# A DiT block in fp32: the projection's seven sums in a ring of two-bank tiles, its rows stored by GpSimd, weight operations spread over groups, three casts on ScalarE

## The chip, the cores and the metric

The program runs on one core of a Trainium2 chip. The metric is device time in microseconds, the median of the runs. Before the change it is 3237.1 us (three runs, 3235.74 to 3239.63). Lower is better.

## The reference

A transformer block with adaptive layer norm. `x` is (2, 2048, 576) in fp32, the conditioning is (2, 576); there are 16 heads of 36 dimensions and an MLP of width 2304.

```python
mod = jax.nn.silu(c) @ w_ada + b_ada
sh_msa, sc_msa, g_msa, sh_mlp, sc_mlp, g_mlp = jnp.split(mod, 6, axis=1)
xn = _ln(x, 1e-06) * (1 + sc_msa[:, None, :]) + sh_msa[:, None, :]
qkv = (xn @ w_qkv + b_qkv).reshape(B, N, 3, H, hd)
q, k, v = _ln(qkv[:, :, 0], ...), _ln(qkv[:, :, 1], ...), qkv[:, :, 2]
attn = softmax(einsum('bqhd,bkhd->bhqk', q, k) * hd ** -0.5)
o = einsum('bhqk,bkhd->bqhd', attn, v).reshape(B, N, C)
x = x + g_msa[:, None, :] * (o @ w_proj + b_proj)
xn2 = _ln(x, 1e-06) * (1 + sc_mlp[:, None, :]) + sh_mlp[:, None, :]
m = gelu(xn2 @ w1 + b1) @ w2 + b2
x = x + g_mlp[:, None, :] * m
```

## The kernel before

For each of the two batches the kernel runs three stages in turn: the QKV product (`inputs`, sixteen tiles of 128 tokens), attention (`attend`) and the output projection (`outputs`). Then one MLP runs over both batches. In the trace batch 0 has its attention until 1034 us and its projection from there to 1139; batch 1 has its projection from 2140 to 2229, and the MLP follows.

**Attention** walks over 8 pairs of heads (p), 4 blocks of 512 queries (qb) and 4 groups of keys (g). Each step of about 6 us makes scores (L1225), their exponentials on ScalarE (L1229) and the product with the values (L1238). VectorE takes that product out of PSUM (L1286 for the first group, L1288 for the others), which frees the bank for the next scores, and at the end of a query block divides by the sums: L1257 is the reciprocal, L1258 the product with it. Work for other stages hangs on this loop as *hooks*, functions called at a given (p, qb, g). `residual_begun` is one: at g = 3 of each query block from p = 3 on, GpSimd adds the gated bias to one tile of `x` and stores it to `x1_dram` (L1409, L1412, L1413). `output_weights` is another: it loads `w_proj`, and three hooks at p = 5 let GpSimd multiply the weights by the gate (`gated`, L1320 and L1323), make three sums (`summed`, L1326 to L1328) and two differences (`differed`, L1331, L1332). A hook only decides the place of its instructions in GpSimd's order.

**Projection.** Eight pairs of token tiles are worked one after the other with Strassen's scheme: a pair's 256 tokens by 512 features against the 512 by 576 weights, in seven products (`product`, L1435) in place of eight, and the last 64 features apart (`last_product`, L1441). GpSimd makes the sums of token blocks that the products need (`pair_summed`, L1371 and L1373), two pairs ahead, in two sets of memory. The products land in three PSUM tiles: `four` of four banks, `two` of two banks and `one` of one bank (two buffers). VectorE adds them into the pair's rows in SBUF, which hold the residual from `residual` (L1427, a load by GpSimd from `x1_dram`): L1458, L1465, L1466, L1467, L1470 and L1479. `inner` are the two middle quarters of the rows and `outer` the first and last. Then SP stores the rows to `x1_dram` (L1480). In batch 0 the rows have five scratch tiles, in batch 1 three, because there the place holds the last 64 rows of `w1`.

In batch 0 five tiles of the finished rows are also normalised and transposed for the MLP: `rows_measured` (L272 to L278) in one pair, L1460 in the next, in place, and the transpose L998 after it. SP loads the weights of batch 1's QKV in this stage (`kept_weights`, L970 to L974). In batch 1 the MLP's work comes in between (`placed`): four sums of weights on VectorE (`weight_sums`, L1663 to L1666), the splitting of the last weight rows into a rounded part and its rest (`last_parts`; `weight_parts`, L400 and L401), and the modulation of tiles (L1020, L388, L389 on ScalarE and L390 on GpSimd).

**Order.** A planner orders the instructions of each engine by its own costs, except inside `manual_schedule`, where program order holds for the engines named: TensorE everywhere in this path, VectorE and GpSimd in attention and in the projection. Semaphores guard what is shared, by tile.

Of the kernel before, what the change touches and what calls it, by code (L numbers as in the profile page):

```python
# [31 lines left out]
def dit_block(  # L32
# [364 lines left out]

    def weight_parts(dst, src):

        nc.vector.tensor_copy(dst[0:64], src)  # L400
        nc.vector.tensor_tensor(dst[64:128], src, dst[0:64].bitcast(F32), ALU.subtract)  # L401
# [350 lines left out]
    def block_of_small():  # L752
# [547 lines left out]
        def output_weights(b):  # L1300
# [16 lines left out]

            def gated():
                for k in range(FULL):
                    nc.gpsimd.tensor_tensor(wp[:, k, :], wp[:, k, :], g1, ALU.mult)  # L1320
                for a in range(2):
                    r = slice(64 * a, 64 * a + 64)
                    nc.gpsimd.tensor_tensor(wp4[r, 0, :], wp4[r, 0, :], g1[r, a * HALF : (a + 1) * HALF], ALU.mult)  # L1323

            def summed():
                nc.gpsimd.tensor_tensor(sums[1], sums[2], sums[5], ALU.add)  # L1326
                nc.gpsimd.tensor_tensor(sums[6], sums[2], sums[3], ALU.add)
                nc.gpsimd.tensor_tensor(sums[7], sums[4], sums[5], ALU.add)  # L1328

            def differed():  # L1330
                nc.gpsimd.tensor_tensor(sums[3], sums[3], sums[5], ALU.subtract)  # L1331
                nc.gpsimd.tensor_tensor(sums[4], sums[4], sums[2], ALU.subtract)  # L1332

            return (sums, wp4[:, 0, :]), (gated, summed, differed), close

# [79 lines left out]
        def outputs(b, weights, memory, between, scratch, turned_of=lambda t: None):  # L1415
# [17 lines left out]
            def product(out, tokens, i, start=True):  # L1433
                for k in range(2):
                    nc.tensor.matmul(  # L1435
                        out[:, :HALF], tokens[:, k, :], sums[i][:, k, :], start=start and k == 0, stop=k == 1
                    )

            def last_product(out, tokens, a):
                r = slice(64 * a, 64 * a + 64)  # L1440
                nc.tensor.matmul(out[:, :HALF], tokens[r], last[r], start=True, stop=False)  # L1441
# [3 lines left out]
            for p in range(pairs):  # L1445
                q00, q01, q10, q11, a, c = pair_blocks(p)
                s = memory[p % 2]
                four = psum["q"].tile([P, 4, 512], F32, tag="q", name="four")
                two = psum["m"].tile([P, 2, 512], F32, tag="m", name="two")
                one = psum["r"].tile([P, 512], F32, tag="r", name="one")  # L1450
                y = rows[p].rearrange("p t (a f) -> p (t a) f", a=2)
                inner, outer = y[:, 1:3, :], y[:, 0::3, :]
                placed(2 * p)
                last_product(four[:, 2, :], a, 1)
                last_product(four[:, 1, :], c, 0)
                product(four[:, 2, :], q00, 3, False)
                product(four[:, 3, :], s[2], 2)
                nc.vector.tensor_tensor(inner, four[:, 2:4, :HALF], inner, ALU.add)  # L1458
                for turn, x1, scales in to_turn:
                    nc.vector.tensor_scalar(x1, x1, *scales, ALU.subtract, ALU.mult)  # L1460
# [9 lines left out]
                nc.vector.tensor_tensor(outer, one[:, :HALF].unsqueeze(1).to_broadcast([P, 2, HALF]), outer, ALU.add)  # L1470
                last_product(two[:, 0, :], s["last"], 0)
                last_product(two[:, 1, :], s["last"], 1)
                product(two[:, 0, :], s[7], 7, False)
                product(two[:, 1, :], s[6], 6, False)
# [5 lines left out]
                nc.sync.dma_start(out=rows_of(x1_dram, p), in_=rows[p])  # L1480
                for i in range(2):
# [15 lines left out]
        for b in range(B):  # L1497
# [77 lines left out]
            close_psum()  # L1575
            close_psum = opened_psum(q=1, m=1, r=2)
            wp, _, close_wp = opening["wp"]
            if b + 1 < B:
# [8 lines left out]
                with tc.manual_schedule(engines={mybir.EngineType.DVE, mybir.EngineType.Pool}):  # L1587
# [64 lines left out]
        for j in range(TPB + 1):  # L1652
# [335 lines left out]
```

## Time and profile before

| What | us |
|---|---|
| Median of three runs | 3237.1 |
| The profiled execution | 3235.03 |
| Its span | 3233.1 |
| TensorE busy | 3145.1 |
| VectorE busy | 1564.9 |
| ScalarE busy | 1471.5 |
| GpSimd busy | 739.2 |

In the lines of the profile PE is TensorE's matmul, PEld its weight load, DVE VectorE, ACT ScalarE, POOL GpSimd and SP the engine that only issues DMAs; a "q" behind a name is the engine's sequencer. L1435 is line 1435 of the kernel. A line of waits reads "who, line, for whom: us in total, times, longest". A line of a timeline reads "start, duration, engine, line, operation, destination<-sources, count", and in brackets how long the engine had been idle before it and what ended that. The windows give each engine's busy time in a stretch, the granted TensorE clock (PEclk, 1.00 is full) and the share of DMA time used.

### The profile page before, as it was taken

Reading aid. Unit: us, or ns where it says so; the run is one execution under the profiler, and the core shown is the slowest. Engines: PE = TensorE matmul, PEld = TensorE weight load, DVE = VectorE, ACT = ScalarE, POOL = GpSimd, SP = SyncE. Lnnn points to the kernel's source line nnn. Section 1 sums busy time; section 2 is a strip of 40 time slices with the busy share of each in tenths; the row PEclk is TensorE's granted clock in tenths of the full one; section 3 lists DMA queues with packets and bytes.
Section 4 is the critical chain, followed back from the end, with each engine's and each line's share of the span. In section 5 each row is a group of like instructions: output and inputs, shape, how many; then the busy total and the mean of one; then the engine's idle time right before and its main releaser. Section 6 shows DMA issues by size and latency. Waiting matters only on the chain.

```text
span 3233.1 us, 46806 instructions
## 1 busy us (share of the span) xinstructions
PE 3145.1 (97%) x17489; PEld 1852.9 (57%) x17489; DVE 1564.9 (48%) x2205; ACT 1471.5 (46%) x2843; POOL 739.2 (23%) x998
## 2 busy tenths in 40 slices
PE   7999999999999699999999999998999999999999
PEld 5873333333333478633333333346888888777777
DVE  6653434444445446434344454346566544454454
ACT  2326666666665023366666656641555652000000
POOL 4640000102212345300001121124333420111121
PEclk9999999999999899999999999999999999999999
DMA  5753222222222556511122212245544533433331
GB/s 151 167 97 83 79 61 51 65 58 63 69 75 59 176 119 124 94 40 39 42 58 70 66 50 72 74 135 169 165 135 136 141 113 114 148 129 113 117 103 38
DMA packets 312598, 311.96 MB, mean 96 GB/s; under 512 B 189865, under 2 KB 243305, under 8 KB 310249
## 3 DMA queue, kind: packets, MB, share of 16 engines
q1 hardware_dynamic: 256320, 201.62, 21.6%
q0 software_dynamic: 40656, 100.16, 12.0%
q10 hardware_dynamic: 15384, 7.08, 0.8%
q8 instruction: 141, 2.31, 0.3%
q14 instruction: 97, 0.79, 0.1%
HBM read 191.80 MB, written 106.45 MB: 92 GB/s over the span
## 4 chain that ended last, share of the span: by engine, by line
PE 92%; DVE 3%; DMA 2%; issue 2%; SPq 0%; ACT 0%; POOL 0%; DVEq 0%; POOLq 0%; ACTq 0%
PE b L1238 28%; PE b L1225 18%; PE s L1900 15%; PE m L1740 11%; PE s L1100 11%; PE m L1754 2%; PE one L1740 2%; PE four L1435 2%; PE s L1102 1%; PE two L1435 1%; DMA qk<-turned_qk 1%; DVE den L1257 1%; DMA xt<-in_x_dram 0%; PE one L1435 0%; DVE ot L1258 0%
## 5 line engine op out<-in xcount | busy, mean ns | idle before, releaser
L1229 ACT ACTIVATE pt<-b 128x512 f32<-128x512 f32 x2048 | 1058.2, 608 | 514.2 <-PE b L1238 299.9
L1238 PE MATMUL b<-pt,vt 128*64 128x512 f32 x4096 | 943.9, 603 | 0.0
L1238 PEld LDWEIGHTS b<-pt,vt 128*64 128x64 f32 x4096 | 273.9, 138 | 591.2 <-issue 452.5
L1225 PE MATMUL b<-qm,km 32*128 32x512 f32 x4096 | 578.9, 616 | 12.0 <-DVE ot L1288 8.9
L1288 DVE TENSOR_TENSOR ot<-b,ot 128x512 f32<-128x512 f32 x192 | 132.7, 691 | 620.3 <-PE b L1238 620.3
L1225 PE MATMUL b<-qe,ke 16*128 16x512 f32 x2048 | 428.2, 791 | 2.6 <-DVE ke L857 2.6
L1100 PE MATMUL s<-wq,xnt 128*128 128x288 f32 x1536 | 403.5, 406 | 2.7 <-ACT xnt L395 2.1
L1225 PEld LDWEIGHTS b<-qm,km 32*128 32x128 f32 x4096 | 193.7, 185 | 291.2 <-ACT pt L1229 211.6
L1900 PE MATMUL s<-ws,as 128*128 128x288 f32 x1440 | 351.8, 406 | 0.0
L1100 PEld LDWEIGHTS s<-wq,xnt 128*128 128x128 f32 x1536 | 280.4, 190 | 65.0 <-ACT xnt L395 1.6
L1900 PEld LDWEIGHTS s<-ws,as 128*128 128x128 f32 x1440 | 273.6, 190 | 75.6
L1257 DVE RECIPROCAL den<-den 128x512 f32<-128x512 f32 x64 | 213.6, 3337 | 2.2 <-DMA den<-den_dram 2.1
L1740 PE MATMUL m<-xnt,wb 128*128 128x256 f32 x864 | 210.9, 380 | 2.8 <-DVE cs L1774 2.8
L1740 PE MATMUL m<-s,wb 128*128 128x256 f32 x864 | 211.0, 380 | 0.0
L1003 POOL DMA_DIRECT2D turned<-squares x212 | 142.6, 679 | 287.7 <-DVE squares L998 281.1
L1286 DVE COPY ot<-b 128x512 f32<-128x512 f32 x64 | 44.3, 692 | 278.8 <-PE b L1238 278.8
L1740 PEld LDWEIGHTS m<-s,wb 128*128 128x128 f32 x864 | 165.0, 191 | 22.8
L1225 PEld LDWEIGHTS b<-qe,ke 16*128 16x128 f32 x2048 | 109.3, 185 | 118.6 <-issue 113.5
L1740 PEld LDWEIGHTS m<-xnt,wb 128*128 128x128 f32 x864 | 159.2, 190 | 22.2 <-DVE cs L1774 3.0
L812 POOL DMA_DIRECT2D km<-qk x56 | 28.1, 502 | 582.0 <-PE b L1225 576.9
L1409 POOL DMA_DIRECT2D spare<-in_x_dram x32 | 17.5, 548 | 609.6 <-DVE met L791 609.6
L1778 ACT ACTIVATE cs<-cs,b_sb 128x512 f32<-128x512 f32 x144 | 98.8, 719 | 114.3 <-DVE cs L1773 92.3
(242 smaller groups left out, 3153.4 us busy)
## 6 DMA issues: line engine op xcount, KB each, us to landing
gelu<-cs SPq DMA_DIRECT2D x144, 256.0 KB
hidden<-gelu SPq DMA_DIRECT2D x16, 2304.0 KB
qk<-turned_qk SPq DMA_DIRECT2D x120, 144.0 KB
qm<-qk SPq DMA_DIRECT2D x256, 64.0 KB
den<-den_dram SPq DMA_DIRECT2D x128, 128.0 KB
turned<-squares POOLq DMA_DIRECT2D x212, 72.0 KB, 2.6
xnt<-turned POOLq DMA_DIRECT2D x54, 256.0 KB, 4.0
spare<-in_x_dram POOLq DMA_DIRECT2D x35, 288.0 KB, 3.1
```

Of the source, the lines that this page charges most:

```text
L1003: queue.dma_start(out=by_square[g], in_=squares[g * SQ : (g + 1) * SQ, :].rearrange("p (k j) -> p k j", j=SQ))
L1100: nc.tensor.matmul(out_a, full[:, k, :], wq[:, k, f], start=k == 0, stop=False)
L1225: nc.tensor.matmul(ps, k[r, keys], q[r, :], start=first, stop=not first)
L1229: nc.scalar.activation(pt[:, h, :], banks[2 * c + h], AF.Exp, scale=SCALE)
L1238: nc.tensor.matmul(acc[64 * h : 64 * h + 64, :], vt[:, v0 : v0 + 64], pt[:, h, :], start=pt is pts[0][0], stop=pt is pts[-1][0],)
L1257: nc.vector.reciprocal(den, den)
L1288: nc.vector.tensor_tensor(ot, acc, ot, ALU.add)
L1435: nc.tensor.matmul(out[:, :HALF], tokens[:, k, :], sums[i][:, k, :], start=start and k == 0, stop=k == 1)
L1740: nc.tensor.matmul(out_m[m], wb[:, slot[m], k, f * P : (f + 1) * P], moving[m](k), start=k == 0 and m in (1, 2, 5, 6), stop=k == 1 and m == 1,
L1754: nc.tensor.matmul(out_m[m], wr[w][:, f * P : (f + 1) * P], a[:, i, t * PAIR : (t + 1) * PAIR], start=False, stop=i == 1 and m != 2,)
L1778: nc.scalar.activation(part, part, AF.Gelu, bias=b1_sb[:, g : g + 1])
L1900: nc.tensor.matmul(ms[m], stationary[m][:, f, :], ws[m][:, f, :], start=(f == 0), stop=(f == HF - 1))
```

## The change

It has four parts. The seven sums of a pair go into four PSUM tiles of two banks, `x`, `y`, `z`, `w`, from one pool of four that turns as a ring and stays open into the QKV product of the next batch; VectorE's six additions become eight, four of them half as wide. GpSimd stores the rows in place of SP. The eleven GpSimd operations on the projection's weights hang on eleven hooks at p = 5 and 6 in place of three. The first step of `weight_parts`, the cast, is done by ScalarE for the MLP's last weight rows.

```diff
-    def weight_parts(dst, src):
+    def weight_parts(dst, src, copy=nc.vector.tensor_copy):
-        nc.vector.tensor_copy(dst[0:64], src)
+        copy(dst[0:64], src)
         nc.vector.tensor_tensor(dst[64:128], src, dst[0:64].bitcast(F32), ALU.subtract)
...
+            making = [
+                *(lambda k=k: gated(k) for k in range(FULL)),
+                *(lambda a=a: last_gated(a) for a in range(2)),
+                lambda: combined(1, 2, ALU.add, 5),
+                lambda: combined(6, 2, ALU.add, 3),
+                lambda: combined(7, 4, ALU.add, 5),
+                lambda: combined(3, 3, ALU.subtract, 5),
+                lambda: combined(4, 4, ALU.subtract, 2),
+            ]
+            return (sums, wp4[:, 0, :]), making, close
...
-                four = psum["q"].tile([P, 4, 512], F32, tag="q", name="four")
-                two = psum["m"].tile([P, 2, 512], F32, tag="m", name="two")
-                one = psum["r"].tile([P, 512], F32, tag="r", name="one")
+                x, y, z, w = (s_tile() for _ in range(4))
...
+                def added(dst, part, op=ALU.add):
+                    nc.vector.tensor_tensor(dst, dst, part, op)
...
-                last_product(four[:, 2, :], a, 1)
-                last_product(four[:, 1, :], c, 0)
-                product(four[:, 2, :], q00, 3, False)
-                product(four[:, 3, :], s[2], 2)
-                nc.vector.tensor_tensor(inner, four[:, 2:4, :HALF], inner, ALU.add)
+                last_product(x[:, 0, :], a, 1)
+                last_product(y[:, 1, :], c, 0)
+                product(x[:, 0, :], q00, 3, False)
+                product(x[:, 1, :], s[2], 2)
+                added(inner, x[:, :, :HALF])
+                added(quarters[:, 3, :], x[:, 0, :HALF])
+                added(quarters[:, 3, :], x[:, 1, :HALF], ALU.subtract)
+                product(y[:, 0, :], s[5], 5)
+                product(y[:, 1, :], q11, 4, False)
                 for turn, x1, scales in to_turn:
                     nc.vector.tensor_scalar(x1, x1, *scales, ALU.subtract, ALU.mult)
                     turn(x1)
                 to_turn.clear()
-                product(four[:, 0, :], s[5], 5)
-                product(four[:, 1, :], q11, 4, False)
-                nc.vector.tensor_tensor(inner, four[:, 0:2, :HALF], inner, ALU.add)
-                nc.vector.tensor_tensor(outer, four[:, 1:3, :HALF], outer, ALU.add)
-                nc.vector.tensor_tensor(outer, outer, four[:, 0::3, :HALF], ALU.subtract)
-                product(one, s[1], 1)
+                added(inner, y[:, :, :HALF])
+                added(quarters[:, 0, :], y[:, 0, :HALF], ALU.subtract)
+                added(quarters[:, 0, :], y[:, 1, :HALF])
+                product(w[:, 0, :], s[1], 1)
                 placed(2 * p + 1)
...
+                added(outer, w[:, 0, :HALF].unsqueeze(1).to_broadcast([P, 2, HALF]))
+                last_product(z[:, 0, :], s["last"], 0)
+                last_product(z[:, 1, :], s["last"], 1)
+                product(z[:, 0, :], s[7], 7, False)
+                product(z[:, 1, :], s[6], 6, False)
...
-                nc.vector.tensor_tensor(outer, two[:, :, :HALF], outer, ALU.add)
-                nc.sync.dma_start(out=rows_of(x1_dram, p), in_=rows[p])
+                added(outer, z[:, :, :HALF])
+                nc.gpsimd.dma_start(out=rows_of(x1_dram, p), in_=rows[p])
...
-            hooks |= {(5, 1 + i, 1): lambda i=i: opening["wp"][1][i]() for i in range(3)}
+            hooks |= {
+                (5 + i // 6, 1 + i % 6 // 2, 1 + i % 2): lambda i=i: opening["wp"][1][i]() for i in range(11)
+            }
...
-            close_psum = opened_psum(q=1, m=1, r=2)
+            close_psum = opened_psum(s=4)
...
-                close_psum()
-                close_psum = opened_psum(s=4)
                 loaded[3] = tile_loaded(x[b + 1, 3 * P : 4 * P, :], nc.gpsimd)
...
-            lambda: weight_parts(wr[0], left),
-            lambda: weight_parts(wr[1], right),
+            lambda: weight_parts(wr[0], left, nc.scalar.copy),
+            lambda: weight_parts(wr[1], right, nc.scalar.copy),
             lambda: nc.vector.tensor_tensor(right, right, left, ALU.subtract),
-            lambda: weight_parts(wr[2], right),
+            lambda: weight_parts(wr[2], right, nc.scalar.copy),
```

More of the change, by code (lines that the diff above doesn't have):

```diff
@@ L1316, in output_weights, with gated, last_gated, combined @@
             }
[L1318 to L1334, printed above, removed]
+            def gated(k):
+                nc.gpsimd.tensor_tensor(wp[:, k, :], wp[:, k, :], g1, ALU.mult)
+            def last_gated(a):
+                r = slice(64 * a, 64 * a + 64)
+                nc.gpsimd.tensor_tensor(wp4[r, 0, :], wp4[r, 0, :], g1[r, a * HALF : (a + 1) * HALF], ALU.mult)
+            def combined(i, one, op, two):
+                nc.gpsimd.tensor_tensor(sums[i], sums[one], sums[two], op)
+            making = [
[8 more added lines that the diff above has]
+            return (sums, wp4[:, 0, :]), making, close
         def pair_memory():
@@ L1447, in outputs @@
                 s = memory[p % 2]
-                four = psum["q"].tile([P, 4, 512], F32, tag="q", name="four")
-                two = psum["m"].tile([P, 2, 512], F32, tag="m", name="two")
-                one = psum["r"].tile([P, 512], F32, tag="r", name="one")
-                y = rows[p].rearrange("p t (a f) -> p (t a) f", a=2)
-                inner, outer = y[:, 1:3, :], y[:, 0::3, :]
-                placed(2 * p)
-                last_product(four[:, 2, :], a, 1)
-                last_product(four[:, 1, :], c, 0)
-                product(four[:, 2, :], q00, 3, False)
-                product(four[:, 3, :], s[2], 2)
-                nc.vector.tensor_tensor(inner, four[:, 2:4, :HALF], inner, ALU.add)
+                x, y, z, w = (s_tile() for _ in range(4))
+                quarters = rows[p].rearrange("p t (a f) -> p (t a) f", a=2)
+                inner, outer = quarters[:, 1:3, :], quarters[:, 0::3, :]
+                def added(dst, part, op=ALU.add):
+                    nc.vector.tensor_tensor(dst, dst, part, op)
+                placed(2 * p)
+                last_product(x[:, 0, :], a, 1)
[7 more added lines that the diff above has]
+                product(y[:, 1, :], q11, 4, False)
                 for turn, x1, scales in to_turn:
@@ L1462, in outputs @@
                 to_turn.clear()
-                product(four[:, 0, :], s[5], 5)
-                product(four[:, 1, :], q11, 4, False)
-                nc.vector.tensor_tensor(inner, four[:, 0:2, :HALF], inner, ALU.add)
-                nc.vector.tensor_tensor(outer, four[:, 1:3, :HALF], outer, ALU.add)
-                nc.vector.tensor_tensor(outer, outer, four[:, 0::3, :HALF], ALU.subtract)
-                product(one, s[1], 1)
-                placed(2 * p + 1)
[L1470 to L1474, printed above, removed]
+                added(inner, y[:, :, :HALF])
+                added(quarters[:, 0, :], y[:, 0, :HALF], ALU.subtract)
+                added(quarters[:, 0, :], y[:, 1, :HALF])
+                product(w[:, 0, :], s[1], 1)
+                placed(2 * p + 1)
+                added(outer, w[:, 0, :HALF].unsqueeze(1).to_broadcast([P, 2, HALF]))
[3 more added lines that the diff above has]
+                product(z[:, 1, :], s[6], 6, False)
                 if p >= 1 and p + 2 < pairs:
```

## The prediction

> **What bounds the kernel now.** I read the page first (engines, then the chain that ended last), then TensorE's waits, then stage windows, then the timeline around each hole.
>
> ```profile
> PE 3145.1 (97%) x17489; PEld 1852.9 (57%) x17489; DVE 1564.9 (48%) x2205; ACT 1471.5 (46%) x2843; POOL 739.2 (23%) x998
> PE 92%; DVE 3%; DMA 2%; issue 2%; SPq 0%; ACT 0%; POOL 0%; DVEq 0%; POOLq 0%; ACTq 0%
> ```
>
> TensorE is the bound; no matmul is removed by the change, so it can win only what TensorE now stands idle (and the slow clock that follows idling). The stages in question are the two projections. The windows give duration and busy time by engine:
>
> ```profile
> core 0: us, PE busy (x) PEld busy (x) DVE busy (x) ACT busy (x) POOL busy (x), PEclk, DMA share, GB/s
> 1034.50:1139.20 104.70, 73.60 (x290) 47.50 (x289) 55.17 (x87) 8.72 (x23) 37.42 (x59) 0.89 0.59 174
> 2140.30:2228.50 88.20, 73.50 (x288) 47.52 (x289) 56.59 (x60) 12.19 (x30) 44.97 (x53) 0.96 0.47 162
> ```
>
> The waits inside the first, and then inside the second:
>
> ```profile
> DVE spare L1460 <- DMA x_dram<-spare: 23.9, 1, 23.9
> PE four L1441 <- issue: 19.7, 1, 19.7
> PE four L1435 <- DVE spare L1458: 9.5, 6, 3.4
> ...
> PE four L1435 <- DVE spare L1458: 11.5, 7, 3.6
> ```
>
> Two holes are seen. One: TensorE writes bank 0 of `four` only after VectorE has read banks 2 and 3 (L1458), in nearly every pair; the two are different banks, so it is the tile that is waited for. Two: one wait of 19.7 us, "issue" being no cause. The timeline names it:
>
> ```profile
> 1055.19 0.57 SPq L970 DMA_DIRECT2D wq<-wq_kept  x1
> 1059.26 22.09 SPq L1480 DMA_DIRECT2D x_dram<-spare  x2
> 1075.74 0.58 DVE L1460 TENSOR_SCALAR spare<-spare,mv,rstd 128x576 f32<-128x576 f32 x1 [23.91 <-DMA x_dram<-spare]
> 1079.33 1.42 PE L1441 MATMUL four<-wp,qo 64*128 64x288 f32 x4 [19.69 <-issue]
> ```
>
> Pair 0's rows (final at 1049.5, L1479) are stored from SP behind 5184 KB of weight loads; L1460 overwrites those rows and waits until 1075.7; L1465 to L1467, which free `four`, are queued behind it, and pair 2's first matmul waits for them. The third hole is in attention, and isn't a wait in the lists:
>
> ```profile
> 758.25 5.50 POOL L1320 TENSOR_TENSOR wp<-wp,gate 128x576 f32<-128x576 f32 x4
> 758.36 6.68 DVE L1258 TENSOR_TENSOR ot<-ot,den 128x512 f32<-128x512 f32 x1
> 765.70 1.22 PE L1225 MATMUL b<-qm,km 32*128 32x512 f32 x1 [3.27 <-DVE ot L1288]
> ...
> 817.61 1.42 POOL L1331 TENSOR_TENSOR wp<-wp 128x576 f32<-128x576 f32 x1
> 817.77 3.18 DVE L1258 TENSOR_TENSOR ot<-ot,den 128x512 f32<-128x512 f32 x1
> 818.98 1.41 POOL L1332 TENSOR_TENSOR wp<-wp 128x576 f32<-128x576 f32 x1
> ```
>
> L1258 normally takes 0.69 us. Beside GpSimd's burst of six (L1320, L1323) it takes 6.68, beside the three (L1326 to L1328) 4.61, beside two 3.18, and L1288, which frees TensorE's bank, comes late.
>
> **Weights one per group.** L1288 and L1286 start every 5.98 us undisturbed, 11.96 for two groups. Across the burst of six it is 19.56 (754.33 to 773.89), of three 15.92, of two 12.85: lost 7.60, 3.96 and 0.89, with the slow clock after the hole in it. Batch 1 shows 19.53, 15.91, 12.84. Together 24.9 us. After the change the eleven operations hang on hooks (p, qb, 1) and (p, qb, 2), but none waits for anything, so GpSimd runs the two of one query block back to back as soon as it is past `residual_begun` of the block before, where today's bursts also start. I therefore cost not singles but bursts of two: four of 1.4 us operations at 0.89 (the third burst's form), one of 64-row operations (two last 1.98 us) at 0 to 0.9, say 0.3, and a lone one at 0 (1.4 us late, while L1288 is due 1.95 us after L1258's start). That is 3.9 a batch. Gain 24.9 - 7.8 = **17**; from 14 (all six groups of a batch at 0.89) to 24.9.
>
> A rule to weigh here: the Trainium skill, "SBUF — State Buffer", "SBUF: two separate sides", says VectorE with two SBUF inputs and GpSimd lock each other out for one whole instruction. Then L1258 could be late by one GpSimd operation only, 1.4 us, bursts would be free, and this edit worth nothing (or, given the 24.9 lost, all of it). The row says 6.68 us for six operations of 7.4: the lock outlasts single operations. I go by the row.
>
> **Ring of two-bank tiles.** Pair's unstalled length: the two 64-row products and the first two products take 2.73 us to the point of the wait (pair start 1090.82; product at 1092.58 plus 0.97), from there 5.90 (1094.66 to 1100.56): 8.63, against 9.74 in steady state. Eight make 69.0. With x, y, z, w every tile is fully written before VectorE reads it, and a tile comes back a pair later. VectorE's cost: six additions of 0.756 (4.54) become four of 0.756 and four of 128x288 at 0.45 (L1907 to L1913): 4.82, and 7.3 with the 2.5 us of measuring and turning in batch 0: below 8.63.
>
> *Batch 0.* Pair 0: 1034.5 to 1043.0 without the wait. VectorE meanwhile has 14 us of work from 1035.3 (three turned tiles 5.0, additions 4.8, L1257 3.35, L1258 0.7), so pair 0's rows are final at 1049.3, as now. GpSimd stores them (0.72 to issue); landing 4 to 5 us, by `spare<-x_dram` loads of the same 576 KB and queue (3.9 to 5.5, with 8.1 for the one issued at 1061.3 beside the weights). So L1460 runs at about 1053.5, before or just as the weights start (1055.2), not at 1075.7. Then L998 and y's three additions: 1056.6. Pair 2's second matmul writes y and would be due at 1053: **3.6 us** remain of the 19.7. From there six pairs less that: end at 1065 + 5 x 8.63 = 1108. Against 1139.2: **31 us**. If the store takes the loaded 8.1: 27. With no hole at all: 35.7.
>
> A rule that speaks against stores on GpSimd: the skill's "SBUF — State Buffer", same section, says GpSimd cannot write a DMA's descriptors while VectorE is in a two-port operation, the form of L1460's tensor_scalar (0.57 us). If it bit, each of the five pairs with an L1460 would be up to 0.6 us later, 3 us if all lay on the path. The issues of L1427 from the same queue last 0.71 to 0.72 us in all eleven cases of these two stages, so I add nothing.
>
> *Batch 1.* Floor again 69.0 of 88.2, at most 19 gained. What stays: (a) start, L1257 waits for its DMA until 2146.2 and y's additions may come behind it: 2 us of p1. (b) p3 to p6: VectorE has 4.8, a weight sum of 2.55 and 1.35 (L401), 8.7 in all, just TensorE's pace; L1664 no longer sits between a pair's own products (it made 3.65 us of hole in p4). About 1 us. (c) GpSimd. With three scratch tiles `residual(p + 2)` waits until the store of pair p - 1 has landed, and store and reload are now both in GpSimd's order: 3.9 landing, 0.7 reload, 4.6 sums (five of 0.72, two of 0.49): 9.2 a pair against 8.63, plus 2 where VectorE's SBUF operations hold it (2.96 and 3.71 us for 0.72 at 2172.8 and 2184.5), plus 4 once beside the w1 loads. Sums are made two pairs ahead, which leaves 6 us: p6 and p7 wait 1 to 2 us. Stage 69 + 4 = 73: gain **15**; from 8 (GpSimd held 4 us in every pair) to 19.
>
> **Casts on ScalarE.** Three casts (1.11, 0.74, 0.74) leave VectorE; ScalarE does each in about 1.15 (128x1152, L1053) while 14% busy there. L401 then waits for ScalarE: for wr0 it waits for its rows' DMA (about 2174) plus 1.15, 2 to 3 us with w's and z's additions behind it; TensorE needs w again 4.6 us into p4. Hidden; without cover 2 us. Counted in (b).
>
> **SP's stores to GpSimd.** SP loses 16 issues of 0.36, GpSimd gains 16 of 0.72: 6.0 a pair in batch 0, covered. The last store stands ahead of the MLP's first row loads on GpSimd; L272 waits 6.5 us for those now and L1774 then holds TensorE 2.8: **-1**.
>
> Sum: 17 + 31 + 15 - 1 = 62. Profiled execution 3235.0 (span 3233.1, 1.9 around it) becomes 3173; the median of the runs lies 2.1 above, so **3175**.
>
> **Rivals.**
> *GpSimd becomes the projection's pace (15%).* For: in-order store, landing, reload, sums. Against: six us of lead. Batch 1 gains 0 to 5, batch 0 some 27: 3188 to 3195.
> *The tile isn't the cause of L1458's wait (8%).* If the ring leaves it, 14 waits of 1.1 us stay; the store and the hooks still give about 17 + 20 + 6: 3194. Against: only same-tile reads precede those waits.
> *Slower (4%).* Stores behind GpSimd's order hold the sums in batch 1 until TensorE starves. It must eat 62 us in the five pairs with a reload, 12 us each: a landing over 16 us. The longest on this queue is 8.1. Price at twice the break-even: 3290.
> The likeliest has 71%, its own range 3160 to 3186; another 2% is a change that does nothing.
>
> **Numbers.** Range for 8 in 10: floor of all three holes 3157, rivals to 3195; 3157 to 3195. A measurement can tell 0.2% (6.5 us) from nothing: faster 0.94, within 0.02, slower 0.04.
>
> **What would show.** Projection windows of 73 to 75 us each; no wait of a product for the first addition; pair starts 8.6 us apart; L1460 waiting 1 to 5 us; L1258 never above 3.3 us, but five bursts of it a batch; TensorE busy unchanged but for the half-clock parts. Wrong if GpSimd's L1371 releases TensorE in most pairs of batch 1, if L1460 waits 10 us or more, or if QKV or MLP begins with a new hole.

## The result and the profile after

The changed kernel takes 3186.1 us (median; 3185.8 to 3188.7) against 3236.4 before, a ratio of 0.985 with a 95% interval of 0.983 to 0.986. The gain is 50 us where 62 were forecast; 3175 was predicted, with 3157 to 3195 as the range. The direction and most terms hold, and one term, batch 0's projection, is wrong by almost half.

The engines and the chain that ended last, on the page of after:

```profile
PE 3137.0 (98%) x17489; PEld 1853.1 (58%) x17489; DVE 1563.2 (49%) x2234; ACT 1474.0 (46%) x2846; POOL 746.4 (23%) x1014
PE 93%; DMA 3%; DVE 1%; POOL 1%; issue 1%; SPq 0%; ACT 0%; ACTq 0%; DVEq 0%; POOLq 0%
```

TensorE's busy time fell by 8 us with the same 17489 products: less of it ran at the slow clock (over the whole span the granted clock is 0.994, and was 0.989); VectorE's share of the chain fell from 3% to 1%, and DMA's rose from 2% to 3%. The line numbers have moved: L1456 is now the one line of all additions, L1438 the products, L1444 the last products, L1469 the normalising in place that was L1460, L1487 the store of rows, L1430 the reload. The windows of the two projections:

```profile
core 0: us, PE busy (x) PEld busy (x) DVE busy (x) ACT busy (x) POOL busy (x), PEclk, DMA share, GB/s
1028.44:1115.66 87.22, 75.72 (x290) 49.98 (x289) 56.36 (x103) 7.32 (x21) 42.24 (x66) 0.90 0.72 209
2106.77:2181.30 74.53, 71.39 (x288) 46.77 (x288) 55.62 (x73) 15.33 (x33) 48.68 (x60) 1.00 0.53 181
```

Against 104.7 and 88.2 before, batch 0 gained 17.5 us (forecast 31) and batch 1 13.7 (forecast 15). The other stretches of the span: the time until batch 0's projection fell from 1034.5 to 1028.4 (6.1), batch 1's QKV and attention from 1001.1 to 991.1 (10.0), and the MLP, in which L1747 waits 2.96 us for L1781 as L1740 waited 2.84 for L1774, is 1.0 longer. 17.5 + 13.7 + 6.1 + 10.0 - 1.0 = 46.3, which is the difference of the two spans, 3233.15 and 3186.89.

**Where batch 0's time stays.** The pairs start at 1028.4, 1037.9, 1046.4, 1062.1, 1081.5 and 1090.1 and then every 8.5 to 8.6 us. So five pairs run at the length forecast (8.63), pair 0 takes 9.4, pair 2 lasts 15.7 and pair 3 19.4. Of the waits in this stage the first shown here is new, and L278's wait for L276 was 2.0 us before, 0.4 at most:

```profile
ACT std L276 <- issue: 16.7, 1, 16.7
...
PE s L1444 <- DVE spare L1456: 11.4, 3, 4.5
DVE spare L1456 <- PE s L1438: 10.9, 11, 2.3
DVE rstd L278 <- ACT std L276: 10.6, 5, 8.9
...
DVE spare L1469 <- DMA x_dram<-spare: 3.0, 1, 3.0
```

The last of them is the wait that was 23.9 us before: 3.0, as the prediction had it (1 to 5). The timeline shows what took its place:

```profile
1044.47 0.73 POOL L1487 DMA_DIRECT2D x_dram<-spare  x1 [4.58 <-DVE spare L1456]
...
1048.33 0.72 DVE L1469 TENSOR_SCALAR spare<-spare,mv,rstd 128x576 f32<-128x576 f32 x1 [3.00 <-DMA x_dram<-spare]
...
1049.25 0.57 SPq L970 DMA_DIRECT2D wq<-wq_kept  x1
1049.89 12.71 ACTq L1003 DMA_DIRECT2D turned<-spare  x4
1051.41 1.32 PE L1444 MATMUL s<-wp,qo 64*128 64x288 f32 x2 [4.22 <-DVE spare L1456]
...
1059.64 0.34 SPq L973 DMA_DIRECT2D bq<-in_b_qkv_dram  x1
...
1062.64 0.29 ACT L276 ACTIVATE std<-mv,eps 128x1 f32<-128x1 f32 x1 [16.74 <-issue]
1062.97 0.17 DVE L278 RECIPROCAL rstd<-std 128x1 f32<-128x1 f32 x1 [8.93 <-ACT std L276]
...
1064.71 0.75 PE L1444 MATMUL s<-wp,qo 64*128 64x288 f32 x2 [2.63 <-DVE spare L1456]
...
1067.65 0.78 DVE L998 STREAM_TRANSPOSE spare<-spare 128x576 f32<-128x576 f32 x1 [2.50 <-DMA turned<-spare]
...
1069.97 1.32 PE L1444 MATMUL s<-wp,qo 64*128 64x288 f32 x2 [4.51 <-DVE spare L1456]
```

The store of pair 0 is issued at 1044.5 and has landed by 1048.3. L1469 runs then, L998 transposes, and ScalarE issues the four stores of the transposed rows (L1003) at 1049.9, 0.6 us after SP began with the 5184 KB of weights. Their issue takes 12.71 us. ScalarE does one thing after another: the root of the next rows (L276) comes only when the issue is over, at 1062.6. VectorE's reciprocal L278 stands waiting 8.9 us for that root, and the additions that free the ring's tiles are queued behind it, so TensorE stops in pair 3. It stops there twice: 2.63 us behind L278, and 4.51 us behind L998, which overwrites the tile that the four stores read and waits 2.50 us until the last of them has landed, at 1067.6. After the 4.2 and 4.5 us stops it runs at half speed for a while (four products of one group take 2.29 us at 1071.23, and 1.13 later). Before the change the same four stores came when SP's weight loads had landed (the last at 1074.2), and were soon issued:

```profile
1077.16 1.99 ACTq L1003 DMA_DIRECT2D turned<-spare  x4
...
1081.95 0.29 ACT L276 ACTIVATE std<-mv,eps 128x1 f32<-128x1 f32 x1 [22.17 <-DVE mv L274]
```

A row of a queue goes from the start of its first issue to the end of its last. In the 12.71 us of after the issues take 0.31, 0.59, 1.03 and 10.65: it is the fourth that is held. So too the 22.09 us of SP's L1480 in before are two issues, of 0.88 and 0.37 us: the second store waited for pair 1's rows, and the first landed at 1075.6.

**The bursts in attention**, on the timeline of after (compare the six of 5.50 and 6.68 us before):

```profile
760.84 2.79 POOL L1319 TENSOR_TENSOR wp<-wp,gate 128x576 f32<-128x576 f32 x2
760.96 3.23 DVE L1258 TENSOR_TENSOR ot<-ot,den 128x512 f32<-128x512 f32 x1
...
810.57 2.03 POOL L1323 TENSOR_TENSOR wp<-wp,gate 64x288 f32<-64x288 f32 x2
810.70 1.24 DVE L1258 TENSOR_TENSOR ot<-ot,den 128x512 f32<-128x512 f32 x1
```

All is as forecast: bursts of two, L1258 at 3.23, 3.22, 3.24 and 3.17 us beside the four of whole tiles, at 1.24 beside the 64-row pair and 1.82 beside the lone one. Two groups across a burst of two take 12.91 and 12.90 us against 11.96, so 0.95 is lost (0.89 forecast) and 0.02 at the 64-row one (0.3 forecast).

### The profile page after: what moved, and what is told of

Read it like the earlier page. It is cut to its first block, busy times and chain, and to the rows that moved or that the text cites. A ratio compares the mean times of both kernels' runs of the same rounds, so it can differ in the third digit from the quotient of the medians.

```text
span 3186.9 us, 46800 instructions
## 1 busy us (share of the span) xinstructions
PE 3137.0 (98%) x17489; PEld 1853.1 (58%) x17489; DVE 1563.2 (49%) x2234; ACT 1474.0 (46%) x2846; POOL 746.4 (23%) x1014
## 3 DMA queue, kind: packets, MB, share of 16 engines
q8 instruction: 140, 2.29, 0.3%
## 4 chain that ended last, share of the span: by engine, by line
PE 93%; DMA 3%; DVE 1%; POOL 1%; issue 1%; SPq 0%; ACT 0%; ACTq 0%; DVEq 0%; POOLq 0%
PE b L1238 29%; PE b L1225 19%; PE s L1907 15%; PE m L1747 11%; PE s L1100 11%; PE m L1761 2%; PE s L1438 2%; PE one L1747 2%; PE s L1102 1%; DMA qk<-turned_qk 1%; DMA turned<-spare 0%; DMA xt<-in_x_dram 0%; DMA x_dram<-spare 0%; PE s L1444 0%; DVE turned_qk L1078 0%
## 5 line engine op out<-in xcount | busy, mean ns | idle before, releaser
L1747 PE MATMUL m<-xnt,wb 128*128 128x256 f32 x864 | 211.9, 381 | 3.9 <-DVE cs L1781 3.0
L1747 PE MATMUL m<-s,wb 128*128 128x256 f32 x864 | 210.0, 379 | 0.0
L1003 POOL DMA_DIRECT2D turned<-squares x212 | 142.5, 678 | 280.3 <-DVE squares L998 262.1
L1747 PEld LDWEIGHTS m<-s,wb 128*128 128x128 f32 x864 | 164.2, 190 | 22.4
L1747 PEld LDWEIGHTS m<-xnt,wb 128*128 128x128 f32 x864 | 159.9, 191 | 23.9 <-DVE cs L1781 3.2
```

Source lines behind the costliest of these rows:

```text
L1003: queue.dma_start(out=by_square[g], in_=squares[g * SQ : (g + 1) * SQ, :].rearrange("p (k j) -> p k j", j=SQ))
L1747: nc.tensor.matmul(out_m[m], wb[:, slot[m], k, f * P : (f + 1) * P], moving[m](k), start=k == 0 and m in (1, 2, 5, 6), stop=k == 1 and m == 1,
```

## The experiments

Theory A: the larger part of batch 0's missing 13.5 us comes from ScalarE's queue. The four stores L1003, now issued beside SP's weight loads, hold ScalarE for 12.7 us, and L276, L278, the additions and TensorE wait in this order. In its wide form these stores are slow to issue from any engine while the loads run; in its narrow form only from ScalarE's queue. Rivals leave that queue out: the busy DMA engines make landings late (L1469's wait and the reloads), or GpSimd's order, longer by the stores, is late with sums. "Stage" is from the first matmul of a projection to the first of the stage after it; by this measure before has 104.9 and 88.4, after 87.2 and 75.5. The ratios are to before, run again beside each group of kernels with medians of 3236.4 to 3239.3; medians of different groups can differ by some 3 us from that alone.

| Kernel | median us | ratio to before | 95% | stage of batch 0 | of batch 1 |
|---|---|---|---|---|---|
| after | 3186.1 | 0.985 | 0.983 to 0.986 | 87.2 | 75.5 |
| weights late | 3176.7 | 0.981 | 0.980 to 0.983 | 76.2 | 74.9 |
| weights in the middle | 3186.0 | 0.984 | 0.982 to 0.986 | 88.7 | 74.5 |
| turned by GpSimd | 3175.5 | 0.981 | 0.979 to 0.983 | 78.3 | 74.9 |
| turn after y, weights late | 3170.8 | 0.979 | 0.978 to 0.981 | 70.2 | 75.5 |
| ring alone | 3207.9 | 0.991 | 0.989 to 0.993 | 97.0 | 71.6 |
| store alone | 3224.6 | 0.996 | 0.994 to 0.997 | 94.5 | 89.5 |
| SP's store back | 3191.0 | 0.985 | 0.983 to 0.988 | 96.4 | 70.5 |
| casts back | 3187.1 | 0.984 | 0.982 to 0.987 | 87.4 | 76.3 |
| one operation per block | 3182.5 | 0.983 | 0.981 to 0.984 | 86.1 | 76.5 |
| combined | 3158.2 | 0.975 | 0.974 to 0.977 | 70.3 | 70.5 |

**Weights late.** SP's five weight loads are issued in the middle of pair 5, after the last rows have been turned. A one-element write by VectorE into each tile keeps SP from starting earlier; nothing else is changed.

```diff
-            nc.sync.dma_start(out=wq[:, :, 0 : 2 * C], in_=saved["wq"])
...
-            return (wq, wq4, bq), close, None
+            def loads():
+                for first in (wq[0:1, 0, 0:1], wq[0:1, 0, 2 * C : 2 * C + 1], wq4.bitcast(F32)[0:1, 0:1]):
+                    nc.vector.memset(first, 0.0)
...
+                nc.sync.dma_start(out=wq[:, :, 0 : 2 * C], in_=saved["wq"])
...
+            return (wq, wq4, bq), close, loads
...
-                        {12: [lambda: input_modulated(b + 1, xnts[0])]},
+                        {11: [loads], 12: [lambda: input_modulated(b + 1, xnts[0])]},
```

> The changed kernel with the loads of batch 1's QKV weights (5184 KB on SP) held back until the middle of projection pair 5 of batch 0, by small writes of VectorE into their tiles. Theory A (ScalarE's four stores of transposed rows, L1003, stand behind these loads for 12.7 us; ScalarE's next root, L276, stands behind the stores; VectorE's L278 waits for it, and TensorE for VectorE): the four stores issue in 2 to 3 us, L278 waits under 1 us, batch 0's projection falls from 87.2 us to 73 to 76, the kernel from 3186 to 3172 to 3176. What stays is the 4 us in pair 2, for the landing of pair 0's store. Theory B (the landing of GpSimd's store is the whole remaining hole): pair 2 still loses 5 to 7 us and pair 3 its 8, stage 84 or more, kernel within 3 us of 3186. Theory C (VectorE has simply too much to do): as B.

The stage falls by 11.0 us and the median by 9.4, both just short of what was expected. The timeline (the lines are 7 further down: L1010 is L1003, L1476 is L1469, L1451 is L1444):

```profile
1046.00 0.75 DVE L1476 TENSOR_SCALAR spare<-spare,mv,rstd 128x576 f32<-128x576 f32 x1 [2.98 <-DMA x_dram<-spare]
...
1047.60 2.13 ACTq L1010 DMA_DIRECT2D turned<-spare  x4
1049.11 1.02 PE L1451 MATMUL s<-wp,qo 64*128 64x288 f32 x2 [4.58 <-DVE spare L1463]
...
1051.78 0.29 ACT L276 ACTIVATE std<-mv,eps 128x1 f32<-128x1 f32 x1 [8.17 <-DVE mv L274]
```

Without the loads the issue takes 2.13 us, L276 waits only for what it needs (L274), and pair 3's hole is gone: the pairs start at 1043.8, 1059.3, 1067.9. The 15.5 us of pair 2 are still there, with L1476 waiting 2.98 for the store. So the two holes have two causes. L1005, the old L998, no longer waits for a landing either.

**Weights in the middle.** The same, with the loads at the start of pair 4 (`{8: [loads], ...}`).

> As above, but the loads are held back only until the start of pair 4, so that they run beside the stores of transposed rows of pairs 4 and 5. Theory A: pairs 1 to 3 run free, the hole moves: a long issue of L1003 in pair 4 or 5, a late L276 and a hole of 5 to 10 us one or two pairs later; stage 78 to 86. Theory B: pairs 2 and 3 keep their holes, no new one. Theory C: no change of place.

No gain: the hole moves with the loads, and the stage is 2.7 over the range expected.

```profile
1069.21 0.57 SPq L976 DMA_DIRECT2D wq<-wq_kept  x1
...
1072.58 11.23 ACTq L1010 DMA_DIRECT2D turned<-spare  x4
...
1083.91 0.29 ACT L276 ACTIVATE std<-mv,eps 128x1 f32<-128x1 f32 x1 [14.99 <-issue]
1084.24 0.17 DVE L278 RECIPROCAL rstd<-std 128x1 f32<-128x1 f32 x1 [7.15 <-ACT std L276]
```

The issue that meets the loads takes 11.23 us, the one before 3.21, the one after 1.99. What decides is not how late the loads are, but whether a pair still has rows to turn beside them.

**Turned by GpSimd.** The loads stay where after has them, and GpSimd issues the four stores of transposed rows.

```diff
-                    return (lambda x1: first.append(squares_turned(x1, nc.scalar, spare[10]))) if t <= TPB else None
+                    return (lambda x1: first.append(squares_turned(x1, nc.gpsimd, spare[10]))) if t <= TPB else None
```

> The changed kernel with the stores of transposed rows in batch 0's projection issued by GpSimd in place of ScalarE; the weight loads stay where they are. Theory A in its narrow form (it is ScalarE's place in the queue that matters): L276 no longer waits, GpSimd's own queue takes 2.7 us for the four stores as it does elsewhere, stage 75 to 80, kernel 3174 to 3180. Theory A in a wide form (any queue's stores of small pieces stall beside the weight loads): GpSimd's issue lasts 8 us or more and its sums come late, stage 85 to 92. Theories B and C: stage as it is, 86 to 88.

```profile
1048.24 0.57 SPq L970 DMA_DIRECT2D wq<-wq_kept  x1
1048.79 2.67 POOL L1003 DMA_DIRECT2D turned<-spare  x4 [4.74 <-DVE spare L998]
...
1051.16 0.95 SPq L974 DMA_DIRECT2D wq<-in_w_qkv_dram  x1
...
1052.69 0.29 ACT L276 ACTIVATE std<-mv,eps 128x1 f32<-128x1 f32 x1 [1.02 <-DVE mv L274]
```

Beside the same loads GpSimd issues the four in 2.67 us, L276 is on time, and L278's waits add up to 2.4 us, 0.4 at most. The stage falls by 8.9 us and the median by 10.7. The narrow form of A holds: the same bytes are stored beside the same loads, and pair 3 takes 8.8 us. Of the rivals, GpSimd's order is out (no product of after's stage waited for GpSimd). Late landings keep a small part: here too L998 waits once 3.0 us for stores to land, and TensorE loses 1.4 by it in pair 4. A by-product: SP's own issues are also over sooner. L974 comes 2.9 us after L970; in after L970 is at 1049.25, L973 at 1059.64 and L974 at 1066.73 (the last section says why).

**Turn after y, weights late.** Beside the late loads, L1469 and the transpose move behind the three additions of `y`.

```diff
+                added(inner, y[:, :, :HALF])
+                added(quarters[:, 0, :], y[:, 0, :HALF], ALU.subtract)
+                added(quarters[:, 0, :], y[:, 1, :HALF])
                 for turn, x1, scales in to_turn:
                     nc.vector.tensor_scalar(x1, x1, *scales, ALU.subtract, ALU.mult)
                     turn(x1)
                 to_turn.clear()
-                added(inner, y[:, :, :HALF])
-                added(quarters[:, 0, :], y[:, 0, :HALF], ALU.subtract)
-                added(quarters[:, 0, :], y[:, 1, :HALF])
```

> The run with the weight loads held back, and in it the normalising and transposing of a finished tile (L1469 and L998 of the changed kernel) put behind y's three additions on VectorE in place of ahead of them. Theory (what is left of the hole in pair 2 is the landing of pair 0's store, with y's bank held behind it): L1469 still waits about 3 us, but y is read before it; pair 2's 6.9 us fall to 0 to 2, batch 0's projection from 76.2 to 69 to 72 us, the kernel 3169 to 3173. If VectorE had too much to do in pair 1 the wait goes to w, and the stage stays at 74 or more.

Against the late loads alone the stage falls by 6.0 us, to 70.2, and the median by 5.9. L1479, the old L1469, still waits 1.4 us for the store, but nothing of pair 1 stands behind it: pair 2 lasts 9.0 in place of 15.5, and TensorE shows no wait for VectorE. This is pair 2's hole, and with pair 3's it makes the whole of what was missing: 87.2 - 11.0 - 6.0 = 70.2, near the prediction's floor of 69.0.

**Ring alone.** After with the store on SP, the operations in three bursts and the casts on VectorE, as before.

```diff
-                nc.gpsimd.dma_start(out=rows_of(x1_dram, p), in_=rows[p])
+                nc.sync.dma_start(out=rows_of(x1_dram, p), in_=rows[p])
...
-                (5 + i // 6, 1 + i % 6 // 2, 1 + i % 2): lambda i=i: opening["wp"][1][i]() for i in range(11)
+                (5, 1 + i, 1): lambda at=at, end=end: bunch(at, end)
+                for i, (at, end) in enumerate(((0, 6), (6, 9), (9, 11)))
...
-            lambda: weight_parts(wr[0], left, nc.scalar.copy),
+            lambda: weight_parts(wr[0], left),
```

> The kernel before with the ring of two-bank tiles and its eight additions alone; stores by SP, three hooks, casts on VectorE as before. If the wait of a product for L1458 comes from the one tile, 13 waits of about 1.1 us go and pairs run at 8.63 us where nothing else holds them; batch 0 keeps the 20 us hole behind SP's weight loads. Batch 0's projection 104.7 to 92 to 97 us, batch 1's 88.2 to 74 to 78, kernel 18 to 26 us below 3236. If the tile isn't the cause the stages stay within 3 us.

31.4 us faster than before in the same runs (3239.3), more than expected. Batch 1's stage falls from 88.4 to 71.6, further than in after (75.5): the tile was indeed the cause of L1458's waits (11.5 us before, one wait of 0.9 for an addition now), and the ring is worth 16.8 us there. Batch 0 gains only 7.9, since the late landing of SP's store is still in it (L1469 waits 23.0 us).

**Store alone.** The kernel before, with only this line changed:

```diff
-                nc.sync.dma_start(out=rows_of(x1_dram, p), in_=rows[p])
+                nc.gpsimd.dma_start(out=rows_of(x1_dram, p), in_=rows[p])
```

> The kernel before with the rows stored by GpSimd alone. If SP's order alone made the 19.7 us hole, batch 0's projection falls by 16 to 20 us. By theory A the wait only changes its place: L1460 runs at once, its stores on ScalarE meet the weight loads, the roots are late: the stage falls by 3 to 9 us only. Batch 1 within 3 us of 88.2. Kernel 3 to 9 us below 3236 by A, 16 to 20 by the other.

L1460's wait falls from 23.9 to 6.0 us, yet the stage of batch 0 falls only from 104.9 to 94.5, as the wait goes where A says:

```profile
1058.60 0.58 DVE L1460 TENSOR_SCALAR spare<-spare,mv,rstd 128x576 f32<-128x576 f32 x1 [6.01 <-DMA x_dram<-spare]
...
1060.02 11.68 ACTq L1003 DMA_DIRECT2D turned<-spare  x4
...
1071.76 0.29 ACT L276 ACTIVATE std<-mv,eps 128x1 f32<-128x1 f32 x1 [18.89 <-issue]
```

So the new wait belongs to the moved store and not to the ring. In batch 1 the store alone makes the stage 1.1 longer. The stage's 10.4 us are near A's range (3 to 9) and far from the other's (16 to 20). The kernel's 14.8 (3239.3 to 3224.6) lie between the two ranges, in part since attention is 3.5 us shorter here, for a reason told under the hooks below.

**SP's store back.** After with that one line turned back.

> The changed kernel with the rows stored by SP again. By theory A the first hole returns in full (L1469 waits until the weight loads are done) but the stores of ScalarE then no longer meet them: one hole of 15 to 20 us in place of two of 7 and 8, batch 0's projection 87 to 95 us. Batch 1 gains a little if GpSimd's order with store and reload was its remaining loss: 71 to 74 us in place of 74.4. Kernel 3184 to 3196. If GpSimd's store is what made the stage faster throughout: 98 us or more.

The waits in batch 0:

```profile
DVE spare L1469 <- DMA x_dram<-spare: 22.7, 1, 22.7
PE s L1444 <- DVE spare L1456: 24.1, 1, 24.1
```

One hole of 24.1 us in place of the two shorter ones; the stage, 96.4, is 1.4 over the range expected. The four stores then take 2.00 us, for they come after the loads. In batch 1 the stage is 70.5, 5.0 better than after. The move of the store to GpSimd is worth 9 us in batch 0 and costs 5 in batch 1; the medians differ by 4.9, with overlapping intervals.

This kernel differs from the ring alone by hooks and casts. Its median is 16.9 lower, and of that the stretches around attention give 6.6 (start of batch 0's projection, 1034.7 to 1028.1) and 6.1 (from the last small products of batch 0's projection to the first of batch 1's, 1000.6 to 994.5).

**Casts back.** `nc.scalar.copy` is taken out of the three calls of `weight_parts`.

> The changed kernel with the three casts of the last weight rows back on VectorE. Forecast was that they are hidden: kernel within 2 us of 3186, batch 1's projection 74 to 77 us. Rival: with VectorE at TensorE's pace in pairs 3 to 6, three casts of 0.74 and what they hold cost 3 to 5 us there.

No difference that can be measured (0.9 us between medians that scatter by 11).

**One operation per block.** Each of the eleven hooks is put into a query block of its own:

```diff
-                (5 + i // 6, 1 + i % 6 // 2, 1 + i % 2): lambda i=i: opening["wp"][1][i]() for i in range(11)
+                (4 + (i + 2) // 4, (i + 2) % 4, 1): lambda i=i: opening["wp"][1][i]() for i in range(11)
```

> The changed kernel with the eleven GpSimd operations on the projection's weights one per query block (p = 4, qb = 2 on to p = 7, qb = 0), so that none follows another back to back. Theory (the loss belongs to bursts: 0.9 us for two operations in a row, nothing for one): L1258 never above 2 us, each of the four bursts of two gains 0.9 us in each batch, kernel 6 to 8 us below 3186. Rival (each operation delays VectorE on its own): eleven small losses in place of six, kernel the same or up to 4 us above.

```profile
712.63 1.43 POOL L1319 TENSOR_TENSOR wp<-wp,gate 128x576 f32<-128x576 f32 x1
712.75 1.87 DVE L1258 TENSOR_TENSOR ot<-ot,den 128x512 f32<-128x512 f32 x1
714.69 0.69 DVE L1288 TENSOR_TENSOR ot<-b,ot 128x512 f32<-128x512 f32 x1
...
928.01 1.43 POOL L1326 TENSOR_TENSOR wp<-wp 128x576 f32<-128x576 f32 x1
929.38 1.41 POOL L1415 TENSOR_TENSOR spare<-spare 128x576 f32<-128x576 f32 x1
```

L1258 falls to 1.83 to 1.92 us beside operations on whole tiles. The last one of each batch still takes 3.22, because L1415, an operation of `residual_begun`, follows L1326 without a gap: two in a row again. The gain is 3.6 us, less than the 6 to 8 expected, and the intervals of the two kernels overlap. The traces tell more than the medians. Added up over the 33 steps from p = 5, qb = 0 to p = 7, qb = 0, the time beyond 5.98 us a step is 3.8 and 2.8 us in the two batches of after, and 1.0 and 1.0 here, 0.9 of it at the one pair that is left. A single operation costs nothing.

**Combined.** Late loads, the turn after `y`, one operation per block, begun one block sooner, and in batch 1 the store on SP:

```diff
-                nc.gpsimd.dma_start(out=rows_of(x1_dram, p), in_=rows[p])
+                (nc.sync if b == B - 1 else nc.gpsimd).dma_start(out=rows_of(x1_dram, p), in_=rows[p])
...
-                (5 + i // 6, 1 + i % 6 // 2, 1 + i % 2): lambda i=i: opening["wp"][1][i]() for i in range(11)
+                (4 + (i + 1) // 4, (i + 1) % 4, 1): lambda i=i: opening["wp"][1][i]() for i in range(11)
```

> All that helped, together: weight loads held back, the turn behind y's additions, SP storing the rows in batch 1 and GpSimd in batch 0, one weight operation per query block from p = 4, qb = 1 to p = 6, qb = 3. By the theories: batch 0's projection 69 to 72 us, batch 1's 70 to 72 in place of 75.5, no L1258 above 2 us, 2 to 4 us less in attention. Kernel 3159 to 3168. If the gains were not independent: 3168 to 3173.

3158.2 us, 28 less than after and 80 less than before in the same runs (3238.3). The windows of the two projections:

```profile
1021.50:1091.72 70.22, 70.08 (x291) 47.06 (x289) 56.48 (x108) 6.09 (x17) 42.34 (x66) 1.00 0.76 221
2079.70:2149.20 69.50, 69.19 (x288) 46.32 (x288) 55.95 (x73) 15.34 (x33) 43.34 (x53) 1.00 0.60 206
```

TensorE is busy in 99.8% and 99.6% of them at the full clock, at the prediction's length of eight unstalled pairs, 69.0. Nothing is left here but the products themselves. In attention no L1258 takes over 1.93 us, and the same 33 steps lose 0.1 us a batch.

## Why the prediction was right or wrong

**Right: the pair's length.** 8.63 us was the forecast of an unstalled pair; after runs 8.5 to 8.6, and the combined kernel's eight make 69.5 to 70.2. The rival that the tile isn't the cause of L1458's wait fell with the ring alone.

**Wrong: batch 0, 31 us.** The step that failed is "From there six pairs less that: end at 1065 + 5 x 8.63 = 1108." The steps before it, about the store, held: issued when pair 0's rows were final, landed 3.9 us later, L1469 waiting 3.0. But the stall was followed only along VectorE, to L1460 and `y`. What L1460 sets going was left out: L998, then four stores in ScalarE's order. With L1460 21 us earlier in the stage (19.9 us after its start, 41.2 before the change) they met the weight loads, which they had missed before. Pair 3 lost 10.8 us (19.4 against 8.63); that it was ScalarE's queue is shown by the GpSimd turn, in which only the issuing engine differs, and by the two kernels that move the loads. Part of the 10.8 came by a second way, the late landing of the same stores, on which L998 waited. The trace of before had the facts: L1003 at 1077 after SP's loads, L276 behind it on the same engine. But it held no example of such an issue beside the loads: the question could have been asked, but the 12.7 us could not have been read.

The other part of the miss is a size. The prediction allowed pair 2 a hole of 3.6 us; TensorE waited 4.2 and then ran at half speed, so that pair 2 was 7.1 too long. Slow products after a hole are to be counted with the hole: the prediction did so for the bursts, not here. In sum: the first three pairs took 33.7 against 30.5 (1034.5 to 1065), pair 3 took 10.8 more than forecast and the last four 0.3 less, 13.7 in all over the 73.5 us between 1034.5 and 1108.

The median, 3186.1, lies in the forecast range all the same, at the end of the likeliest case's own 3160 to 3186. The range went on to 3195 for two rivals, and neither came true; the miss has a cause that no rival named. That the range held is in part luck.

The Trainium skill, "DMA: Bandwidth & Descriptors", "Issuing engines are not separate DMA queues", says that issuing from several engines saves only the sequencer's time to initiate a DMA, usually small beside the DMA. Read by it alone, moving L1003 from ScalarE to GpSimd would be worth at most the 2 us of issue that ScalarE had before; it was worth 10.7 us of the whole. The row that decides is 12.71 us against 2.67 for the same four stores.

**About right, in part by luck: batch 1, 15 us forecast, 13.7 measured.** Two terms were wrong in opposite ways. The first pairs are nearly free (8.5, 9.6, 8.6, 8.6: 0.8 over the floor for (a) and (b), 3 allowed), and the last four lose 4.7 (9.3, 9.8, 11.2, 9.0), where (c) had 1 to 2. The mechanism of (c) is the predicted one, seen in GpSimd's timeline:

```profile
2128.30 0.74 POOL L1487 DMA_DIRECT2D x_dram<-spare  x1
2137.07 0.72 POOL L1430 DMA_DIRECT2D spare<-x_dram  x1 [8.04 <-DMA x_dram<-spare]
...
2163.26 3.08 POOL L1374 TENSOR_TENSOR x_first<-qo 128x256 f32<-128x256 f32 x1
...
2166.39 1.24 PE L1438 MATMUL s<-wp,x_first 128*128 128x288 f32 x4 [1.79 <-POOL x_first L1374]
```

The store must land before the reload may be issued, once 8.0 us and then 1.0, 2.4 and 2.4 in GpSimd's order, and single sums of 0.72 us are stretched to 2.4, 1.9 and 3.1. The lead of two pairs is used up by pair 5. With the store on SP this stage is 5.0 us shorter, which is the whole of (c). The rival that GpSimd becomes the pace, with only 0 to 5 us gained in batch 1, did not come true: what it names cost some 5 us of the 19 to be had. (In the prediction's reading of GpSimd's stretched sums, the 3.71 us at 2184.5 are two sums, of 0.72 and 3.03.)

**Right: the hooks, 17 us.** The same 33 steps of attention lost 12.5 and 12.4 us in before, the 24.9 that the prediction added up, and 3.8 and 2.8 in after: 18.3 us are gained. The two stretches around the projections gave 16.1, but they hold other things too: the first step of a batch's attention varies by 3 us from profile to profile. The loss itself isn't quite steady. With the old hooks ring alone lost 10.4 in batch 1 and store alone 8.6, where the burst of three met no L1258 at all. That is most of the 3 us by which their second stretch is shorter than in before (1003.7 to 1000.6 and 1000.2).

The rule of single operations that was weighed did not fall; the conclusion did, that it would make bursts free. In every row L1258 ends 0.55 or 0.56 us after a GpSimd operation: after one (1.87 us), the second of two (3.23), the third of three (4.61), the fifth of six (6.68). The whole-tile operations of a burst are recorded as overlapping by some 0.05 us, so between them there is no moment for VectorE. The 64-row ones lie 0.07 us apart, and there L1258 comes in after the first of two (1.24) and after the fifth of the six. A lock of one instruction each fits these rows. The records of GpSimd are rough, so the overlap is a reading, and only the lengths of L1258 are sure.

**Right: the casts.** They are worth nothing, as forecast. GpSimd's issues of stores and reloads lasted 0.71 to 0.74 us everywhere in these stages, so nothing was to be added for the rule that speaks against its stores.

**Right by luck: start of the MLP, 1 us forecast, 1.0 measured.** The wait that the prediction meant, L1774's, grew only by 0.1 us, 2.84 to 2.96. (The store does weigh on it: 3.47 with the store alone, 1.93 in after with SP's store.) The 1.0 us is another wait, ahead of the MLP's first product, with no cause in the profile:

```profile
2182.29 1.97 PE L1747 MATMUL m<-xnt,wb 128*128 128x256 f32 x8 [0.89 <-issue]
```

Ring alone and SP's store back have the same 0.89 us, before and store alone have none, so it comes with the ring and not with GpSimd's store.

## What to carry to other kernels

When a wait is taken away, follow everything that the released instruction sets going, on every engine and queue, to the place in time where it now falls: what it avoided before by being late, it may meet now. An engine that both computes and issues DMAs can be stopped for as long as its issues take, and so can all who wait for its small results; such stores belong on an engine with no result due, or away from large loads. An operation that waits for a transfer goes behind the work that frees buffers, not ahead of it. GpSimd operations that may meet VectorE's go singly, not in bursts.

## What the runs showed of the hardware that was not expected

Four stores of 72 KB, in pieces of 128 bytes, took 11.23 to 13.14 us to issue from ScalarE in the five kernels where they met SP's first weight loads, 1.99 to 3.7 us without these loads, and 2.67 us from GpSimd beside the loads. What holds the fourth issue is open. In after it wasn't a semaphore: the one it uses was free at 1051.6, before the issue began. Nor are loads beside it enough, or a full queue: the next four stores, at 1068.46, took 2.74 us beside the last load (1152 KB), and none of their packets had started by then. In the first case the DMA engines were working on all three queues. From 1052.6 to 1062.6 they started 629 packets of SP's, 210 of GpSimd's and only 561 of ScalarE's; in before, with nothing else under way, 2368 of ScalarE's took 4 us (1077 to 1081). That only the issuing engine had to change is shown.

SP's own later issues in after were held by something else, and this the trace settles. Each DMA has a semaphore that tells of its landing. SP and ScalarE take theirs in this program from the same eight, GpSimd from eight others, and an issue waits until the DMA that used its semaphore last has landed. L973 has the semaphore of L970, which was complete at 1059.63, and starts at 1059.64; L974 has that of ScalarE's second store, complete at 1066.72, and starts at 1066.73. In the other four kernels with the long issue SP's loads wait in the same way and start 0.01 to 0.02 us after such a landing. With the stores on GpSimd, SP's five loads find five free semaphores and start within 2.9 us. So a small store that lands late can hold up the issue of a load on another engine's queue that has nothing to do with it.

VectorE's operation with two SBUF inputs is held for a whole run of GpSimd operations on 128x576 that follow each other without a gap, and not only for the first, also when the second comes from another piece of work, as L1415 behind L1326 (3.22 us). Between two 64-row operations, 0.07 us apart, it came in (1.24).
